# Four-layer hybrid network on one core: layer 1's input sent into the residual stream, the order at the begin of its MLP, and Fourier's row and last unit

## The chip, the cores and the metric

The kernel runs on one core of one Trainium2 chip. The metric is the time of one execution on the device, in microseconds; the time before is the median of three runs. The profile is that of one execution, and times inside it count from its first instruction.

## The reference

The input x is (4, 96, 64, 64) float32: batch, channels, image. As the kernel keeps it, it is 96 channels by 4 x 4096 tokens. Four layers follow each other. Layers 2 and 3 add their two parts to the stream of tokens.

```python
x = L0(x)   # two Mamba blocks, a 1x1 fusion with pooled channels, batch norm over (0, 2, 3), + input
x = L1(x)   # depthwise 7x7 conv, layer norm over channels, Linear(96, 384), GELU, Linear(384, 96), scale, + input
t = tokens(x)
t = t + linear_attention(ln(t))
t = t + qffn(ln(t))          # fp8 (e5m2) operands, f16 sums
t = t + fourier(ln(t))       # Linear(96, 192) + BN + ReLU, FFT over 4096 tokens, a complex gate with
                             # ReLU on both parts, inverse FFT, real part, Linear(192, 96), BN
t = t + qffn(ln(t))
```

## The kernel before

The program is one sequence of stages, each with pools of SBUF and PSUM buffers of its own. A pool that is closed gives its memory to the pools opened later; what is written there first waits for the last users of what lay there. Inside a stage the order of PE, DVE, ACT and POOL is the order of the program text (`manual_schedule(engines=...)`). SP, which issues all DMAs, isn't among those engines: a planner puts its instructions in an order of its own, and at run time its queue is strictly in that order, so a DMA that waits holds up all behind it.

**Layer 0** (0 to 2604 us) leaves its result, before the batch norm's scale, in a DRAM tensor `scratch` [96, 16384]. At its end it works out the batch norm's scale and shift, `osc` and `osh` (L614 to L622), in tiles of its pool.

**The turn of layer 1** (L727 to L757). The residual stream `t` [96, 16384] is a tile that lives from here to the end of the kernel; its memory was layer 0's. For each of 16 chunks of 1024 tokens, `tokens` loads a chunk of `scratch` into `o` (three buffers) and a chunk of x into `xr` (three buffers), ACT does o * osc + osh (L736), DVE adds xr and writes t (L737). `turn` then transposes the chunk, 128 tokens at a time, by a matmul with t as the stationary operand (96 rows by 128 columns) and the identity, 96 by 96, as the moving one (L744): eight matmuls a chunk, each of two records in the profile, since they are fp32. Four of them share a PSUM tile, which ACT (L750) or DVE (L748) copies into `xt`, the image with tokens in the partitions. `tokens` runs one chunk ahead of `turn`.

**The convolution** (L760 to L797, 2670 to 2790 us) takes 24 groups of four channels with weights `band` of 1 MB a group. In its ninth group `consts2` loads and prepares the constants of the later stages.

**Layer 1's MLP** (L805 to L870). `stats(k, d)` takes mean and variance of four rows of 128 tokens on DVE (bn_stats, bn_aggr; L810, L811), four such calls make a group k of 16 rows; `roots(k)` makes 1/sqrt on ACT with Ln and Exp; `back(i)` normalizes four rows (L824) and turns them back to channels on PE (L829), into `xc`; `hidden(i)` is the first linear with GELU (L838, L839), `out(i)` the second with the addition to t (L844, L847). There are 32 units i, in eight groups k. Before the first `hidden`, the kernel does the statistics and roots of groups 0 and 1 and `back` of units 0 to 3.

**Fourier** (`fourier`). A unit u is one image and one half of the 192 hidden channels: eight units. An iteration j takes a sixth part of a quarter of them, 6 groups of 4 channels, so that each unit has four iterations (`PER`), and the steps of several parts are staggered: `over_n1(j)` (first DFT, L1139), `over_n2(j-1)` (second DFT and gate, L1160 to L1179), `fold(j-2)`, `over_k2(j-3)` (first inverse DFT, L1208 to L1210, which fills the tile `bt[u]`). Frequency 64 is kept apart: `row64(u)` (L1216 to L1223) computes its 24 by 128 values, ACT copies them to `r`, a DMA writes them to DRAM (`d<-r`), and a second DMA loads them as row 64 of `bt[u]` (`bt<-d`). It is called in iteration 4u + 7. From iteration 4u + 8 on, the eight blocks of unit u are done, two an iteration: `over_k1` (second inverse DFT, L1230, with a table `gt` of 256 KB loaded for each block into one of two buffers, and ACT's copy to `ys`, L1232), then `w2` (the last linear, L1238, and the addition to t, L1242 or L1244). In the remaining places of an iteration stand the layer norm of the next image (`norm1`, `norm2`) and its first linear (`w1`, L1125), which are there only for the first three images. Most of the small matmuls share the two PSUM buffers of `misc`.

```python
                    if (j - 7) % PER == 0 and 0 <= (j - 7) // PER < len(units):
                        row64((j - 7) // PER)
```

The last FFN (`qffn`, 3838 us to the end) follows.

Of the kernel before, what the change touches and what calls it, by code (L numbers as in the profile page):

```python
# [9 lines left out]
F32 = mybir.dt.float32  # L10
# [8 lines left out]
B, C, HW, L = 4, 96, 64, 4096  # L19
# [31 lines left out]
class Net:  # L51
# [661 lines left out]
    def layer1(self, scratch, t):  # L713
# [4 lines left out]
        with ExitStack() as ctx:  # L718
            xpool = ctx.enter_context(tc.tile_pool(name="l1x", bufs=1))
            xt = xpool.tile([128, C, B, NR + 4], F32, name="xt")  # L720
            cb = xpool.tile([128, C], F32, name="cb")
            nc.sync.dma_start(cb, ins["c_b_row"].partition_broadcast(128))
            with (
                tc.manual_schedule(engines=engines),
                tc.tile_pool(name="l1a", bufs=1) as wk,
                tc.tile_pool(name="l1ap", bufs=1, space=PSUM) as psum,
            ):  # L727
                for at in (slice(0, 2), slice(NR + 2, NR + 4)):
                    nc.gpsimd.memset(xt[:, :, :, at], 0.0)
                def tokens(b, s):  # L730
                    at = slice(b * L + s * T, b * L + (s + 1) * T)
                    o = wk.tile([C, T], F32, name="o", tag="o", bufs=3)
                    nc.sync.dma_start(o, scratch[:, at])
                    xr = wk.tile([C, T], F32, name="xr", tag="xr", bufs=3)
                    nc.sync.dma_start(xr, ins["x"][b, :, s * T : (s + 1) * T])
                    nc.scalar.activation(o, o, AF.Identity, scale=self.osc, bias=self.osh)  # L736
                    nc.vector.tensor_add(t[:, at], o, xr)  # L737

                def turn(b, s):
                    for h in range(2):  # L740
                        ps = psum.tile([128, 4, C], F32, name="xt_ps", tag="xt", bufs=4)
                        for d in range(4):
                            a = b * L + s * T + (4 * h + d) * 128
                            nc.tensor.matmul(ps[:, d], t[:, a : a + 128], self.ident[:C, :C], start=True, stop=True)  # L744
                        r = 2 + s * (T // 128) + 4 * h
                        dst = xt[:, :, b, r : r + 4].rearrange("p c r -> p r c")
                        if h:
                            nc.vector.tensor_copy(dst, ps)  # L748
                        else:
                            nc.scalar.copy(dst, ps)  # L750

                chunks = [(b, s) for b in range(B) for s in range(NSC)]
                tokens(*chunks[0])
                for k, chunk in enumerate(chunks):
                    if k + 1 < len(chunks):
                        tokens(*chunks[k + 1])
                    turn(*chunk)  # L757

                def load(g):
                    w = wk.tile([128, GC, 4, 128], F32, name="band", tag="band", bufs=3)  # L760
                    nc.sync.dma_start(w, ins["band"][g])
                    return w

                def outer(g):

                    x2 = wk.tile([128, 2 * GC, B, NR], F32, name="x2", tag="x2", bufs=3)
                    at = slice(g * 2 * GC, (g + 1) * 2 * GC)
                    nc.gpsimd.tensor_copy(x2[:64], xt[:64, at, :, 4:])
                    nc.gpsimd.tensor_copy(x2[64:], xt[64:, at, :, :NR])
                    return x2  # L770

                def small(rows, cols):
                    ps = psum.tile([128, 4, C], F32, name="w_ps", tag="xt", bufs=4)
                    return ps.rearrange("p a c -> p (a c)")[:rows, :cols]

                x2 = [outer(0)]
                for g in range(C // GC):
                    if g == 8:
                        self.consts2(wk, small)
                    if g % 2 == 0 and g + 2 < C // GC:  # L780
                        x2.append(outer(g // 2 + 1))
                    w = load(g)
                    ps = psum.tile([128, GC, B, NR], F32, name="cv_ps", tag="cv", bufs=4)
                    for d in range(GC):
                        c = g * GC + d
                        for k, j in enumerate((1, 0, 2)):
                            nc.tensor.matmul(
                                ps[:, d], w[:, d, j], xt[:, c, :, 1 + j : 1 + j + NR], start=k == 0, stop=False
                            )
                        nc.tensor.matmul(ps[:, d], w[:, d, 3], x2[g // 2][:, g % 2 * GC + d], start=False, stop=True)  # L790
                    for d in range(GC):
                        c = g * GC + d
                        dst = xt[:, c, :, 2 : 2 + NR]
                        if g % 2:
                            nc.vector.tensor_scalar_add(dst, ps[:, d], cb[:, c : c + 1])
                        else:
                            nc.scalar.activation(dst, ps[:, d], AF.Identity, bias=cb[:, c : c + 1])  # L797
# [52 lines left out]
            n = NT // MB // 4  # L850
            with tc.manual_schedule(engines=engines):
                nc.scalar.preload_act_table_set(ACT_EXP_LN)
                for k in range(2):
                    for d in range(4):
                        stats(k, d)
                    roots(k)
                for d in range(4):
                    back(d)
                for k in range(n):
                    for d in range(4):  # L860
                        hidden(4 * k + d)
                        if k + 1 < n:
                            back(4 * k + 4 + d)
                        if k + 2 < n:
                            stats(k + 2, d)
                        if d:
                            out(4 * k + d - 1)
                    if k + 2 < n:
                        nc.scalar.preload_act_table_set(ACT_EXP_LN)
                        roots(k + 2)  # L870
                    out(4 * k + 3)
# [212 lines left out]
    def fourier(self, dram, t, h):  # L1084
# [5 lines left out]
        with ExitStack() as ctx:  # L1090
# [107 lines left out]
            def over_k2(i):  # L1198

                u, g = its[i]  # L1200
                z = zz.pop(i)
                if g == 0:
                    bt[u] = wk.tile([N1, N2, C], F32, name="bt", tag="bt", bufs=2)
                for e in range(0, G, 3):
                    ps = pln.tile([N1, 3, 128], F32, name="i1_ps", tag="i1", bufs=2)
                    for d in range(3):
                        zd = z[:, e + d].rearrange("p k m -> p (k m)")
                        nc.tensor.matmul(ps[:, d], zd[:, 64:], bc, start=True, stop=False)  # L1208
                        nc.tensor.matmul(ps[:, d], zd[:, :128], bs, start=False, stop=True)  # L1209
                    nc.scalar.copy(  # L1210
                        bt[u].rearrange("p n (g c) -> p g n c", c=4)[:, g + e : g + e + 3],
                        ps.rearrange("p g (n c) -> p g n c", c=4),
                    )

            def row64(u):
# [6 lines left out]
                nc.sync.dma_start(d.rearrange("o (n g c) -> g (o n) c", n=N2, c=4), r)  # L1222
                nc.sync.dma_start(bt[u][64:65].rearrange("p n c -> p (n c)"), d)  # L1223

            def over_k1(u, n, kept):
                gt = wk.tile([N1, 4, N1], F32, name="gt", tag="gt", bufs=2)
                nc.sync.dma_start(gt, ins["idft"][:, n : n + 4])
                ps = misc(C).rearrange("p (n a) -> p n a", n=4)
                for d in range(4):
                    nc.tensor.matmul(ps[:, d], bt[u][:, n + d], gt[:, d], start=True, stop=True)  # L1230
                kept[u, n] = wk.tile([C, MB], F32, name="ys", tag="ys", bufs=2)
                nc.scalar.copy(kept[u, n], ps.rearrange("p n a -> p (n a)"))  # L1232

            def w2(u, n, kept):

                b, half = units[u]
                ps = misc(C)
                nc.tensor.matmul(ps, self.a_w2[:, half, :], kept.pop((u, n)), start=True, stop=True)  # L1238
                ps = ps.rearrange("p (n a) -> p n a", n=4)
                td = ft[b][:, n : n + 4]  # L1240
# [6 lines left out]
            with tc.manual_schedule(engines=engines):  # L1247
                for n in range(0, N2, 2):
                    w1(0, n)
                kept, sq = {}, {}  # L1250
                for j in range(len(its) + 12):
                    ub, k = divmod(j - 2 * PER, PER)
                    blocks = [(ub, n) for n in (8 * k, 8 * k + 4)] if 0 <= ub < len(units) else []

# [9 lines left out]

                    if j < len(its):
                        over_n1(j)

                    if normed:
                        norm1(b, a, sq)
# [18 lines left out]
                        over_k2(j - 3)  # L1288
                    if normed:
                        norm2(a, sq)  # L1290
                    if (j - 7) % PER == 0 and 0 <= (j - 7) // PER < len(units):
                        row64((j - 7) // PER)
                    turn(len(tokens))
                    if blocks:
                        w2(*blocks[1], kept)
                    if normed and k == PER - 1:
                        norm2(a + MB, sq)


def build(tc, ins, out):  # L1300
# [155 lines left out]
```

## Time and profile before

| | |
|---|---|
| median of three runs | 3974.91 us (3973.95 to 3976.82) |
| the profiled execution | 3972.29 us, span 3970.5 us |
| granted TensorE clock, mean | 0.858 |
| layer 1: turn | 2614.6 to 2669.3 us |
| layer 1: convolution | 2670.4 to 2790.6 us |
| layer 1: MLP | 2790.7 to 3011.2 us |
| layer 3: Fourier, first L1139 to the last addition to t | 3318.1 to 3838.1 us |
| last FFN | 3838.1 us to the end |

The stages from the turn on follow each other on PE, which has work in nearly all of them; the table's times are those at which its first matmul begins or its last result is written. A row of the timeline gives start, duration, engine, line, operation, output and inputs, shapes, the count of instructions merged into it, and in brackets how long the engine was idle before it and what released it.

### The profile page before, as it was taken

To read this page: it belongs to the slowest core of one execution; us is meant where nothing else is said; L and a number is where in the kernel's file an instruction comes from. 1 tells how busy PE (TensorE), PEld (TensorE's weight loads), DVE (VectorE), ACT (ScalarE), POOL (GpSimd) and SP (SyncE) were. 2 spreads that over 40 slices of the span, in tenths; PEclk is the share of its full clock that TensorE was granted. 3 is DMA by queue.
4 is the path that set the end of the run, shared out by engine and by line. 5 is a ranking of instruction groups with operands and counts; after the bars stand their busy time and mean duration, and the time that the engine had idled before them with its cause. 6 is when DMAs were issued, how large, how long until landed. Compare 5 with 4: busy or idle time off the path is not lost. (4 is left out here: it accounts for less than half of the span.)

```text
span 3970.5 us, 45322 instructions
## 1 busy us (share of the span) xinstructions
PE 3291.6 (83%) x14174; PEld 1420.1 (36%) x14174; DVE 3155.9 (79%) x2772; ACT 2419.9 (61%) x4644; POOL 2912.9 (73%) x1443
## 2 busy tenths in 40 slices
PE   7888788888888778888878888677899998999878
PEld 3222222222222222222222222167445535666643
DVE  5999999999999999999999999941662384444539
ACT  4676667666666766677666666431345586655548
POOL 2999999999999999999999999911001064534417
PEclk8888888888887888788888888658899999999989
DMA  7567656756675667566666766566000000011111
GB/s 185 135 161 174 144 148 159 175 142 159 160 173 132 164 166 170 132 167 166 159 147 158 170 148 154 120 170 227 11 0 1 1 1 6 22 33 33 43 44 58
DMA packets 183291, 468.12 MB, mean 118 GB/s; under 512 B 53237, under 2 KB 55167, under 8 KB 179969
## 3 DMA queue, kind: packets, MB, share of 16 engines
q1 hardware_dynamic: 183048, 465.21, 47.1%
q8 instruction: 113, 1.85, 0.2%
q14 instruction: 130, 1.06, 0.1%
HBM read 391.53 MB, written 73.50 MB: 117 GB/s over the span
## 5 line engine op out<-in xcount | busy, mean ns | idle before, releaser
L496 POOL TENSOR_TENSOR hs<-hs,crep 128x1024 f32<-128x1024 f32 x768 | 1796.6, 2364 | 27.3 <-DVE hs L490 23.7
L454 PE MATMUL rep<-dbl,sel_b 32*128 32x512 f32 x1152 | 406.1, 781 | 464.1 <-DVE hs L490 433.4
L474 POOL TENSOR_TENSOR up<-udb,brep 128x1024 f32<-128x1024 f32 x256 | 605.1, 2364 | 8.5 <-DMA brep<-cd 8.5
L468 ACT ACTIVATE da<-ddb,nega 128x1024 f32<-128x1024 f32 x512 | 585.0, 1150 | 16.2 <-DVE hs L490 8.2
L468 ACT ACTIVATE dap<-ddb,nega 128x1024 f32<-128x1024 f32 x256 | 286.2, 1118 | 423.7 <-DVE hs L490 421.9
L515 PE MATMUL y<-hs,sel_r 128*32 128x512 f32 x3072 | 483.3, 689 | 6.5 <-POOL hs L496 6.4
L490 DVE TENSOR_TENSOR_SCAN hs<-da,state,rep 128x1024 f32<-128x1024 f32 x192 | 450.8, 2348 | 16.7
L490 DVE TENSOR_TENSOR_SCAN hs<-da,state,u 128x1024 f32<-128x1024 f32 x192 | 450.9, 2348 | 11.2 <-DVE u L486 1.4
L490 DVE TENSOR_TENSOR_SCAN hs<-dap,state,up 128x1024 f32<-128x1024 f32 x192 | 447.0, 2328 | 6.8 <-ACT dap L468 6.8
L454 PEld LDWEIGHTS rep<-dbl,sel_b 32*128 32x128 f32 x1152 | 109.0, 218 | 760.9 <-issue 512.8
L210 PE MATMUL ps<-n,w_x 97*64 97x512 f32 x1536 | 364.8, 617 | 9.4 <-ACT n L323 5.3
L486 DVE TENSOR_TENSOR u<-udb,rep 128x1024 f32<-128x1024 f32 x256 | 314.6, 1229 | 42.5 <-PE rep L454 11.3
L486 DVE TENSOR_TENSOR rep<-udb,rep 128x1024 f32<-128x1024 f32 x256 | 310.6, 1213 | 0.4
L1039 POOL CAST hq<-y 128x1536 fp8e5<-128x1536 f16 x64 | 93.9, 1467 | 253.7 <-issue 144.0
L210 PEld LDWEIGHTS ps<-n,w_x 97*64 97x64 f32 x1536 | 108.9, 140 | 257.5 <-issue 210.9
L515 PEld LDWEIGHTS y<-hs,sel_r 128*32 128x32 f32 x3072 | 66.9, 116 | 363.5 <-issue 195.8
L382 POOL TENSOR_TENSOR du<-delta,xc 128x512 f32<-128x512 f32 x96 | 122.6, 1277 | 67.4 <-ACT delta L366 52.2
L1178 POOL TENSOR_TENSOR av<-av,ec 128x780 f32<-128x780 f32 x32 | 58.8, 1837 | 150.1 <-ACT av L1175 150.1
L224 PE MATMUL ps<-xc,xproj 64*102 64x512 f32 x384 | 160.3, 998 | 3.5 <-ACT xc L344 3.5
L358 ACT COPY dbl<-ps 102x512 f32<-102x512 f32 x64 | 34.4, 589 | 207.1 <-PE ps L224 207.1
L911 POOL MEMSET h<- 1x4096 f32 x1 | 3.5, 3506 | 213.1 <-DVE n L824 213.1
L490 DVE TENSOR_TENSOR_SCAN hs<-da,rep 128x1024 f32<-128x1024 f32 x64 | 146.5, 2289 | 5.4
(256 smaller groups left out, 6492.9 us busy)
## 6 DMA issues: line engine op xcount, KB each, us to landing
ddb<-dd SPq DMA_DIRECT2D x768, 128.0 KB
udb<-ud SPq DMA_DIRECT2D x768, 128.0 KB
crep<-cd SPq DMA_DIRECT2D x512, 128.0 KB
brep<-cd SPq DMA_DIRECT2D x256, 128.0 KB
dd<-delta SPq DMA_DIRECT2D x64, 384.0 KB
ud<-du SPq DMA_DIRECT2D x192, 128.0 KB
band<-in_band SPq DMA_DIRECT2D x24, 1024.0 KB
gt<-in_idft SPq DMA_DIRECT2D x64, 256.0 KB
```

Source lines behind the costliest of these rows:

```text
L210: nc.tensor.matmul(ps[rows], w[:, 64 * p : 64 * p + 64], rhs[:, at.start + shift : at.stop + shift], start=k == 0, stop=k == len(ws) - 1, ...
L224: nc.tensor.matmul(ps, w[rows, p], x[rows, p], start=start and p == 0, stop=p == 2)
L382: nc.gpsimd.tensor_mul(u, m["delta"][:, of], m["xc"][:, of])
L454: nc.tensor.matmul(x[:, at], sel_b[rows, order[t][1]], made[k]["dbl"][rows, at], start=True, stop=True)
L468: nc.scalar.activation(da, made[k]["dd", h, j], AF.Exp, scale=nega[:, col : col + 1])
L474: nc.gpsimd.tensor_mul(u, made[k]["ud", h, j], made[k]["brep", g])
L486: nc.vector.tensor_mul(u, made[k]["ud", h, j], x)
L490: nc.vector.tensor_tensor_scan(hs[:, 1:], made[k].pop(("da", t)), u, 0.0 if s == 0 else st, ALU.mult, ALU.add)
L496: nc.gpsimd.tensor_mul(hs[:, :T], hs[:, 1:], made[k]["crep", order[t][1]])
L515: nc.tensor.matmul(made[k]["y", p][row : row + 32], sel_r, made[k]["hs", t][:, at], start=False, stop=True, skip_group_check=True,)
L1039: nc.gpsimd.tensor_copy(q, y2, saturate=False)
L1178: nc.gpsimd.tensor_add(v[:, 2:4], v[:, 0:2], ec)
```

## The change

In the turn, x is loaded into t itself, one image (1536 KB) a DMA: images 0 to 2 ahead of all chunks in the program text, image 3 in the fourth chunk's `tokens`. `xr` is gone, DVE adds o to t in place, and o has six buffers. The transposing matmul takes all 128 columns of the identity's first 96 rows; the PSUM tile is one of 4 x 128 columns, and the copies read 96 of each 128.

In the MLP, only the statistics and roots of group 0 and `back(0)` stand before the first `hidden`. `back` runs two units ahead, and in group 0 the statistics of groups 1 and 2 are done at two calls a unit; the roots of group 1 come behind the third `hidden`.

In Fourier, `row64(u)` is called in iteration 4u + 6. The last unit's blocks stand in a loop of their own at the end, with `over_k1` of a block ahead of `w2` of the one before it; the tables are loaded in two DMAs of 1 MB into buffers of `hh`, called in iterations 25 and 29, and from then on each block whose table is there reads it (two blocks of unit 4, all of units 5, 6 and 7) in place of loading `gt`; the last unit's `w2` uses the PSUM buffers of `over_k2` in place of `misc`.

```diff
+            def input_of(b):
+                nc.sync.dma_start(t[:, b * L : (b + 1) * L], ins["x"][b])
+
+            for b in range(B - 1):
+                input_of(b)
...
-                    o = wk.tile([C, T], F32, name="o", tag="o", bufs=3)
+                    o = wk.tile([C, T], F32, name="o", tag="o", bufs=6)
                     nc.sync.dma_start(o, scratch[:, at])
-                    xr = wk.tile([C, T], F32, name="xr", tag="xr", bufs=3)
-                    nc.sync.dma_start(xr, ins["x"][b, :, s * T : (s + 1) * T])
+                    if (b, s) == (0, NSC - 1):
+                        input_of(B - 1)
                     nc.scalar.activation(o, o, AF.Identity, scale=self.osc, bias=self.osh)
-                    nc.vector.tensor_add(t[:, at], o, xr)
+                    nc.vector.tensor_add(t[:, at], o, t[:, at])
...
-                        ps = psum.tile([128, 4, C], F32, name="xt_ps", tag="xt", bufs=4)
+                        ps = psum.tile([128, 4, 128], F32, name="xt_ps", tag="xt", bufs=4)
...
-                            nc.tensor.matmul(ps[:, d], t[:, a : a + 128], self.ident[:C, :C], start=True, stop=True)
+                            nc.tensor.matmul(ps[:, d], t[:, a : a + 128], self.ident[:C], start=True, stop=True)
...
-                            nc.vector.tensor_copy(dst, ps)
+                            nc.vector.tensor_copy(dst, ps[:, :, :C])
                         else:
-                            nc.scalar.copy(dst, ps)
+                            nc.scalar.copy(dst, ps[:, :, :C])
...
-                for k in range(2):
-                    for d in range(4):
-                        stats(k, d)
-                    roots(k)
                 for d in range(4):
-                    back(d)
+                    stats(0, d)
+                roots(0)
+                back(0)
                 for k in range(n):
                     for d in range(4):
-                        hidden(4 * k + d)
-                        if k + 1 < n:
-                            back(4 * k + 4 + d)
-                        if k + 2 < n:
+                        i = 4 * k + d
+                        hidden(i)
+                        if k == 0 and d == 2:
+                            nc.scalar.preload_act_table_set(ACT_EXP_LN)
+                            roots(1)
+                        for i2 in (1, 2) if i == 0 else (i + 2,):
+                            if i2 < 4 * n:
+                                back(i2)
+
+                        if k == 0:
+                            for d2 in (2 * (d % 2), 2 * (d % 2) + 1):
+                                stats(1 + d // 2, d2)
+                        elif k + 2 < n:
                             stats(k + 2, d)
                         if d:
-                            out(4 * k + d - 1)
+                            out(i - 1)
...
+            late = {}
+
+            def fetch(k):
+
+                g = wk.tile([N1, CG, N2, 4], F32, name="hh", tag="hh", bufs=3)
+                g = g.rearrange("p g n c -> p (g n c)")[:, : N2 // 2 * N1].rearrange("p (n a) -> p n a", n=N2 // 2)
+                nc.sync.dma_start(g, ins["idft"][:, k * N2 // 2 : (k + 1) * N2 // 2])
+                for n in range(0, N2 // 2, 4):
+                    late[k * N2 // 2 + n] = g[:, n : n + 4]
+
             def over_k1(u, n, kept):
-                gt = wk.tile([N1, 4, N1], F32, name="gt", tag="gt", bufs=2)
-                nc.sync.dma_start(gt, ins["idft"][:, n : n + 4])
+                if n in late:
+                    gt = late[n]
+                else:
+                    gt = wk.tile([N1, 4, N1], F32, name="gt", tag="gt", bufs=2)
+                    nc.sync.dma_start(gt, ins["idft"][:, n : n + 4])
...
-                ps = misc(C)
+                if u < len(units) - 1:
+                    ps = misc(C)
+                else:
+                    ps = pln.tile([N1, 4, 128], F32, name="i1_ps", tag="i1", bufs=2)[:C].rearrange("p n a -> p (n a)")
...
-                for j in range(len(its) + 12):
+                for j in range(len(its) + 4):
...
                     if j < len(its):
                         over_n1(j)
+                    if j in (len(its) - 7, len(its) - 3):
+                        fetch((j - len(its) + 7) // 4)
...
-                    if (j - 7) % PER == 0 and 0 <= (j - 7) // PER < len(units):
-                        row64((j - 7) // PER)
+                    if (j - 6) % PER == 0 and 0 <= (j - 6) // PER < len(units):
+                        row64((j - 6) // PER)
...
+                last = [(len(units) - 1, n) for n in range(0, N2, 4)]
+                for k, block in enumerate(last):
+                    over_k1(*block, kept)
+                    if k:
+                        w2(*last[k - 1], kept)
+                w2(*last[-1], kept)
```

More of the change, by code (lines that the diff above doesn't have):

```diff
@@ L772, in small @@
                 def small(rows, cols):
-                    ps = psum.tile([128, 4, C], F32, name="w_ps", tag="xt", bufs=4)
+                    ps = psum.tile([128, 4, 128], F32, name="w_ps", tag="xt", bufs=4)
                     return ps.rearrange("p a c -> p (a c)")[:rows, :cols]
@@ L1204, in over_k2 @@
                 for e in range(0, G, 3):
-                    ps = pln.tile([N1, 3, 128], F32, name="i1_ps", tag="i1", bufs=2)
+                    ps = pln.tile([N1, 4, 128], F32, name="i1_ps", tag="i1", bufs=2)[:, :3]
                     for d in range(3):
```

## The prediction

> **What bounds the kernel now.** I read the page first (busy shares, the 40 slices), then the busy time by stage, then the timeline around each edit, engine by engine.
>
> ```profile
> PE 3291.6 (83%) x14174; PEld 1420.1 (36%) x14174; DVE 3155.9 (79%) x2772; ACT 2419.9 (61%) x4644; POOL 2912.9 (73%) x1443
> PEclk8888888888887888788888888658899999999989
> ```
>
> The shares say little: layer 0, 0 to 2604 us, is bound by DVE and POOL and is not edited. What the change touches lies behind 2604, where PE leads; slices 27 and 28 have a granted clock of 0.6 and 0.5. By stage:
>
> ```profile
> 2614.50:2640.00 25.50, 25.42 (x119) 25.42 (x120) 13.74 (x16) 14.52 (x15) 0.00 (x0) 0.50 1.02 262
> 2740.00:2780.00 40.00, 40.00 (x360) 40.00 (x360) 6.19 (x23) 6.87 (x24) 9.81 (x10) 1.00 0.87 293
> ```
>
> Columns after the length: busy PE, PEld, DVE, ACT, POOL, then clock, DMA share, GB/s. The first row is layer 1's turn (L744): PE is full, but at half clock, and the DMA engines are full too, at 262 GB/s. The second is the convolution: PE full at full clock. The turn runs from 2614.58 to 2669.3, 256 matmul records in 54.7 us, 213 ns each.
>
> In Fourier, the waits of PE at the first block of a unit:
>
> ```profile
> 3477.94 1.94 PE L1230 MATMUL m_ps<-gt,bt 128*96 128x128 f32 x8 [2.95 <-DMA bt<-d]
> ...
> 3605.41 1.99 PE L1230 MATMUL m_ps<-gt,bt 128*96 128x128 f32 x8 [3.20 <-issue]
> ...
> 3719.93 1.60 PE L1230 MATMUL m_ps<-gt,bt 128*96 128x128 f32 x8 [3.55 <-DMA bt<-d]
> ...
> 3770.96 1.99 PE L1230 MATMUL m_ps<-gt,bt 128*96 128x128 f32 x8 [4.89 <-DMA bt<-d]
> ...
> 3812.57 1.99 PE L1230 MATMUL m_ps<-gt,bt 128*96 128x128 f32 x8 [4.73 <-issue]
> ```
>
> Brackets: idle before, and who ended it. With 0.83 (3543.39) and 1.66 (3670.59) these are seven waits, 21.8 us, for the row of frequency 64, which goes through DRAM (d<-r, then bt<-d). And the eight matmuls take 1.94 to 1.99 us there, 1.04 elsewhere: the clock has fallen. The last unit, in PE's timeline:
>
> ```profile
> 3822.44 1.10 PE L1238 MATMUL m_ps<-ys,a_w2s 96*96 96x512 f32 x2 [0.72 <-ACT ys L1232]
> 3823.38 1.04 PE L1230 MATMUL m_ps<-gt,bt 128*96 128x128 f32 x8
> 3825.14 1.10 PE L1238 MATMUL m_ps<-ys,a_w2s 96*96 96x512 f32 x2 [0.73 <-ACT ys L1232]
> ```
>
> A block is 2.70 us: PE, ACT's copy, PE, with nothing between. And the begin of the MLP:
>
> ```profile
> 2804.67 1.99 PE L829 MATMUL tp_ps<-ident,n 128*96 128x128 f32 x8 [15.28 <-DVE n L824]
> ```
>
> PE waits for 32 rows of statistics.
>
> **What the Trainium skill says.** "TensorE: Matmul & The Clock Gate", section "What's actually happening": the array's clock is half until it has been busy for a window of about 3.4 us, and falls back after an idle one. The trace agrees: the convolution goes from 0.51 (2670 to 2676) to 1.00, and waits of 2.95 us and more are followed by half speed; also waits of under 1 us at 3485, so the rule is not the whole of it. The same page, "LDWEIGHTS (loading the stationary operand)": the load's time goes by the columns of the stationary tile. Here that is 128, and L744's 213 ns (96 moving columns) is the pace of L829 at half clock with 128 moving columns (8 in 1.99 us): 128 columns should cost L744 nothing. "DMA: Bandwidth & Descriptors", section "Why a DMA increments its semaphore by 16 and not by 1": 96 rows go over all 16 engines, 97 over one. Trace: o and xr (96 rows) reach 262 GB/s, bn1_rows (97 rows, 291 KB, issued at 2695.72, used at 2717.29) takes 21.6 us.
>
> **Part A, input and turn.** Gone: 16 transfers xr of 384 KB. New: four of 1536 KB into t, by the same queue, SP's. Same bytes: 12.6 MB in all. SP is not ordered by hand; t stands where layer 0's pool stood, which is read until L622 (2609.4). So I take SP's order as: six o (six buffers now), then x0 to x3, then o6. In front of x0 are cb, the last store and six o, 2.8 MB; from 2605.5 at 260 GB/s to 2616.3; x0 6 us, to 2622.3; landing takes 1 to 2 more (xr0 was seen to land only at 2613.2, behind 1.2 MB). First add and matmul at about 2625, 10 us later than now. x1 to x3 come at 2630, 2636, 2642, o6, stuck behind them, at 2643.5. Chunks 0 to 5 are through by then (at full clock 1.8 us each); chunk 6 waits. From there a chunk costs ACT 1.23 + 0.80 = 2.03 us, DVE 1.20 + 0.80 = 2.00, PE 16 x 0.111 = 1.78 (the convolution's pitch): nine more to 2662, the last matmul at about 2665, against 2669.3: **-4**. The convolution begins at a warmer clock: its first group took 5.8 us, of which 2.2 wait for POOL, 3.58 is the later pace: **-1**. Bounds: at 310 GB/s, seen from 2607 to 2608.5, x0 lands 4 us sooner and o6 7 sooner: -12. At half clock: 2625 + 54.7 = 2679.7: +10. That the clock rises isn't shown for this shape; I take it, since 128 moving columns leave no hole in the array's stream where 96 leave a quarter. Queued behind: the bands, issued after the last o; 3.1 MB at 416 GB/s (2660 to 2664) is 7.6 us, hidden by the rest of the turn.
>
> **Part B, begin of the MLP.** DVE ends the convolution at 2790.6; 16 statistics x 0.42 = 6.7, roots with two table loads 3.15: first matmul at 2801.3, 3.4 sooner. Then PE waits more: 0.9 for the first xc, 1.2 before the third turn, 2.0 before the fourth (eight statistics, 3.4 us, lie in front on DVE), 3.3 before the fifth (table load 1.28, roots 0.53, behind the third unit's Gelu): 7.4, against 3.6 now. Three turns get full clock, 1.1 each, but 3.3 us of idleness may take the clock away again, 2 to 3 us. PE's work, 32 x (0.87 + 6 x 0.86) = 193 us, is the same. Sum: -3.4 + 3.8 - 3.3 + 2.5: **0**, bounds -4 and +3.
>
> **Part C, the row.** row64 moves from iteration 4u+7 to 4u+6, behind the unit's last over_k2; with it PE's four matmuls, ACT's copy and both DMAs. Their chain, 5.6 us (d<-r 3.0, bt<-d 2.4), then has an iteration of 11.6 to 14.7 us as cover, in the last unit two w2 and two blocks, 6 us. SP: both stand between gt transfers whose blocks are one iteration off. What a wait costs shows in the iterations, from L1139 to L1139:
>
> ```profile
> 3473.48 1.50 PE L1139 MATMUL s_ps<-dft,hh 128*128 128x130 f32 x12
> ...
> 3495.48 1.50 PE L1139 MATMUL s_ps<-dft,hh 128*128 128x130 f32 x12
> ...
> 3510.14 1.50 PE L1139 MATMUL s_ps<-dft,hh 128*128 128x130 f32 x12
> ```
>
> 22.0 us with the wait, 14.66 without. I leave 0.65 for small waits: 6.7 for unit 1, 6.5 for unit 3 (21.82). Unit 5: 15.58 against 11.58, 4.0. Units 2 and 4: 0.8 each. Unit 6: 4.89 and 2.1 of half clock, less 0.6 since ACT's fold then comes in front: 6.4. Unit 7: 4.6 and 2.7 of half clock (0.95, 0.92, 0.87): 7.3. Sum 32.5, less 1.5 for what comes next (ACT's ys): **-31**. Bounds: the bare waits, -20, and -34.
>
> **Part D, last unit.** over_k1 of a block now runs ahead of w2 of the one before: 0.87 + 0.86 = 1.73 us a block on PE, over ACT's 0.58 + 0.15 and DVE's 1.15. 8 x (2.70 - 1.73) = 7.8, less 0.3 at the ends: **-7.5**. It needs gt early: two loads of 1 MB (2.6 us each at 416 GB/s), called in iterations 25 and 29, in hh buffers last read in 23 and 27. Every block from then on whose part is there uses it: two of unit 4, all of units 5 to 7, so 26 loads of 256 KB go, 6.8 MB for 2. On SP the two hold up a row or gt for 2.6 us at most, inside the slack. The first readers stand in iterations 25 and 30; if SP puts a load late, PE waits up to 4 us there (2.6 and a landing); SP may put it as early as the buffer is free, so 0. The last FFN then begins at a warmer clock: its first iterations take 4.4 us with 2.02 for L887, 1.10 later: 0 to -4, I take **-1**.
>
> Other edits (PSUM shapes of 128 columns, one bank as before): nothing.
>
> **Sum.** -5 + 0 - 31 - 7.5 - 1 = -44.5. From the profiled execution's 3972.3 (span 3970.5) 3927.8; the median, 3974.9, lies 2.6 higher: **3930**.
>
> **Rivals.**
> 1. The turn stays at half clock: part A +10 in place of -5: 3945. For it: 54 us at 0.50 with PE full; against: the convolution, of 128 columns, goes to 1.00.
> 2. Only the waits go, the half clock stays (as at 3485, without a long wait): part C -20: 3941. Against: the iterations without a row wait have 1.00.
> 3. Long rows are quick, 310 GB/s, and the clock rises: part A -12: 3923.
> 4. Slower: t's rows are 16 KB, a length that no load around here has. bn1_rows shows what few engines mean: 291 KB in 21.6 us, 13.5 GB/s on one. If x fell to few engines, its 6.3 MB would hold all o behind it: on one engine 466 us, some 4370 in all. It decides from the point where the 6.3 MB take the 24 us planned here and the 40 us gained elsewhere: 98 GB/s, seven such engines. Against it: xr, also 96 rows, runs at 262 GB/s.
>
> **Numbers.** Likeliest 0.62; rival 1 0.13; 2 0.12; 3 0.09; 4 0.04. A measurement here can tell some 0.2%, 8 us. All but rival 4 are faster by more; I leave 0.03 for no change. The range 3912 to 3949 holds the first, rivals 1 to 3, and their bounds in part.
>
> **What would show it.** Right: L744 at 111 ns a record and a clock near 1.00 in the turn, its first matmul near 2625 and a wait of a few us at the seventh chunk; L1230 with no wait for bt<-d; iterations 12 and 20 under 16 us; blocks of the last unit of 1.75 us. Wrong: L744 at 213 ns; PE waiting over 3 us at L1230 for gt or bt; the first matmul of the turn after 2635; an MLP that ends over 3 us sooner or later against its begin.

## The result, and the profile after

The changed kernel takes 3938.60 us (median of four runs, 3937.12 to 3940.83), beside 3974.43 us of the kernel before: ratio 0.9916, interval 0.9896 to 0.9935. That is 33 us less by the ratio (26 to 41 by its interval) and 36 by the two medians; the forecast was 45, with 26 to 63 as its range. The profiled execution takes 3937.12 us (span 3935.4), 35.2 less than that of before. The total lies in the range; several of its parts don't lie where they were put, and one gain was not in the sum at all.

The page of the kernel after, its busy times and clock slices:

```profile
PE 3262.6 (83%) x14174; PEld 1392.3 (35%) x14174; DVE 3156.6 (80%) x2772; ACT 2418.7 (61%) x4644; POOL 2912.1 (74%) x1443
PEclk8788878888888888888898888768899999999999
```

PE has the same 14174 matmuls in 29 us less busy time, 17.7 us of it in the turn, where they had run at half clock. The slices around the turn stand at 7 and 6 where 6 and 5 stood.

By stages, from the two traces (the end of each is where the next one's first matmul starts, for the convolution the start of its last matmul, for Fourier the end of the last addition to t):

| stage | before, us | after, us | difference |
|---|---|---|---|
| to the end of the turn (of it, layer 0 is 1.5 shorter) | 2670.4 | 2674.6 | +4.2 |
| convolution | 118.7 | 114.0 | -4.7 |
| layer 1's MLP | 222.1 | 222.8 | +0.7 |
| attention, first FFN | 306.8 | 299.8 | -7.0 |
| Fourier | 520.0 | 491.3 | -28.7 |
| last FFN | 132.4 | 132.8 | +0.4 |

**The turn.** PE's timeline of the kernel after (start, duration, line, in brackets the wait and its releaser):

```profile
2621.19 8.20 PE L750 MATMUL xt_ps<-ident,t 96*128 96x128 f32 x48 [18.40 <-DVE t L743]
2637.58 3.79 PE L750 MATMUL xt_ps<-ident,t 96*128 96x128 f32 x16 [8.19 <-DVE t L743]
2645.91 7.81 PE L750 MATMUL xt_ps<-ident,t 96*128 96x128 f32 x48 [4.54 <-DVE t L743]
2654.23 3.84 PE L750 MATMUL xt_ps<-ident,t 96*128 96x128 f32 x32 [0.52 <-DVE t L743]
```

And SP's queue, where a row's duration reaches over all issues merged into it:

```profile
2605.31 0.94 SPq L739 DMA_DIRECT2D o<-scratch  x2
2609.87 1.26 SPq L725 DMA_DIRECT2D t<-in_x  x3
2611.17 0.42 SPq L739 DMA_DIRECT2D o<-scratch  x1
2611.64 0.69 SPq L725 DMA_DIRECT2D t<-in_x  x1
2612.36 46.49 SPq L739 DMA_DIRECT2D o<-scratch  x12
```

Three chunks of o (the first was issued at 2603.38) are ahead of x; then three images, 4.7 MB, then the fourth o, then the last image, and then the other twelve o. The fourth chunk (16 records) waits until 2637.58, the fifth until 2645.91. Behind that, the last two rows are quick: 32 records in 3.84 us and a wait of half a microsecond. In the table of windows the clock is back:

```profile
2655.00:2673.00 18.00, 15.97 (x136) 15.21 (x135) 15.25 (x16) 13.72 (x16) 0.00 (x0) 1.00 0.85 282
```

**The convolution.** Its waits, as total, times and longest, in the kernel after:

```profile
PE w_ps L703 <- DVE bn_d L699: 10.0, 1, 10.0
PE cv_ps L793 <- DMA band<-in_band: 9.6, 3, 8.7
```

Before, the first of these is 25.7 us. bn_rows is issued at 2672.21 now, at 2695.72 before, because SP's order puts the constants right behind the first bands; in return one band comes 8.7 us late.

**The attention,** which no edit touches, begins at full clock in the kernel after, and did not before. First the timeline after, then before, some 1.8 us after the first matmul of the stage in both:

```profile
3013.21 1.10 PE L900 MATMUL v_ps<-sq,ones 96*96 96x512 f32 x2 [0.74 <-ACT sq L896]
3016.23 1.10 PE L900 MATMUL v_ps<-sq,ones 96*96 96x512 f32 x2 [1.06 <-ACT sq L896]
```

```profile
3013.06 1.35 PE L887 MATMUL v_ps<-sq,ones 96*96 96x512 f32 x2 [0.74 <-ACT sq L883]
3016.80 2.02 PE L887 MATMUL v_ps<-sq,ones 96*96 96x512 f32 x2 [0.68 <-ACT sq L883]
```

**Fourier.** No wait for bt<-d is left in the trace. But iterations 12 and 20, from L1152 to L1152, take 18.52 and 19.54 us; an iteration without a wait takes 14.66. All engines of iteration 12 in the timeline after:

```profile
3469.44 1.04 PE L1256 MATMUL m_ps<-gt,bt 128*96 128x128 f32 x8
...
3471.03 1.27 POOL L1129 TENSOR_TENSOR h<-h,ln_rs 96x512 f32<-96x512 f32 x1 [1.46 <-ACT ln_rs L1128]
...
3471.81 2.72 DVE L1203 SCALAR_TENSOR_TENSOR zz<-av 128x384 f32<-128x384 f32 x1 [0.27 <-ACT av L1198]
3472.26 1.86 POOL L1164 TENSOR_TENSOR f<-p,p 128x390 f32<-128x390 f32 x2
...
3474.54 0.55 DVE L1203 SCALAR_TENSOR_TENSOR zz<-av 128x384 f32<-128x384 f32 x1
...
3475.12 0.52 ACT L1209 ACTIVATE zz<-zz 128x384 f32<-128x384 f32 x1 [3.41 <-DVE zz L1203]
3475.55 0.56 ACT L1258 COPY ys<-m_ps 96x512 f32<-96x512 f32 x1
...
3476.16 1.68 PE L1267 MATMUL m_ps<-ys,a_w2s 96*96 96x512 f32 x2 [3.06 <-ACT ys L1258]
3477.64 1.91 PE L1256 MATMUL m_ps<-gt,bt 128*96 128x128 f32 x8
```

To be read from below: w2 waits 3.06 us for ys; the matmul that ys copies ended at 3470.48, but ACT stood in front of it at the fold's last step, 3.41 us, for DVE's zz; of two equal zz, the first took 2.72 us and the second 0.55; and while the first ran, POOL ran too, until 3474.12. The first zz had started 0.45 us before POOL's two f, and still ended only after them. The last row shows what follows a wait of 3 us: eight matmuls at 1.91 us in place of 1.04.

These are figures of one execution. Two other profiles below hold the same Fourier program: there iterations 12 and 20 take 20.10 and 19.50 us, and 20.29 and 18.45, and Fourier takes 492.7 and 494.4 us. Three profiles with the Fourier program of before have 520.1, 516.5 and 517.1. A difference of 2 us in one of these iterations, or of 3 us in the stage, can therefore not be put down to an edit.

**The last unit** runs as forecast, a block every 1.73 us:

```profile
3789.68 1.04 PE L1256 MATMUL m_ps<-hh,bt 128*96 128x128 f32 x8
3790.55 1.02 PE L1267 MATMUL i_ps<-ys,a_w2s 96*96 96x512 f32 x2
3791.41 1.04 PE L1256 MATMUL m_ps<-hh,bt 128*96 128x128 f32 x8
```

### The profile page after: what moved, and what is told of

Its sections match the earlier page's. It is cut to its first block, busy times and chain, and to the rows that moved or that the text cites. A ratio compares the mean times of both kernels' runs of the same rounds, so it can differ in the third digit from the quotient of the medians.

```text
span 3935.4 us, 45230 instructions
## 1 busy us (share of the span) xinstructions
PE 3262.6 (83%) x14174; PEld 1392.3 (35%) x14174; DVE 3156.6 (80%) x2772; ACT 2418.7 (61%) x4644; POOL 2912.1 (74%) x1443
```

## The experiments

Twelve further kernels ran in three rounds, each with the kernel before beside it (its medians 3972.30, 3971.97, 3972.89).

| kernel | median, us | ratio to before, interval |
|---|---|---|
| 128 columns alone | 3964.35 | 0.9981 (0.9974 to 0.9987) |
| input part alone | 3977.43 | 1.0013 (1.0006 to 1.0019) |
| MLP's begin alone | 3965.53 | 0.9985 (0.9979 to 0.9992) |
| row64 alone | 3956.60 | 0.9959 (0.9947 to 0.9970) |
| last unit alone | 3957.73 | 0.9965 (0.9953 to 0.9978) |
| after, without the input part | 3928.73 | 0.9897 (0.9882 to 0.9913) |
| after, old begin of the MLP | 3946.58 | 0.9931 (0.9918 to 0.9944) |
| after, POOL's sums moved | 3935.60 | 0.9908 (0.9894 to 0.9922) |
| after, over_k1 ahead of fold | 3928.88 | 0.9895 (0.9880 to 0.9911) |
| after, fold ahead of over_n1 | 3929.36 | 0.9896 (0.9878 to 0.9914) |
| no input part, over_k1 ahead of fold | 3915.37 | 0.9860 (0.9846 to 0.9875) |
| no input part, order over_k1, fold, over_n1 | 3895.21 | 0.9809 (0.9791 to 0.9826) |

The five parts alone sum to -40 us by their medians, which the interval of the whole change, 26 to 41 us, holds. A kernel that differs from the changed one by 10 us or less has an interval that overlaps with the changed one's; there the reading rests on the stages of the profiles.

### Which half of part A costs, which gains?

The kernel before with 128 columns only:

```diff
-ps = psum.tile([128, 4, C], F32, name="xt_ps", tag="xt", bufs=4)
+ps = psum.tile([128, 4, 128], F32, name="xt_ps", tag="xt", bufs=4)
-nc.tensor.matmul(ps[:, d], t[:, a : a + 128], self.ident[:C, :C], start=True, stop=True)
+nc.tensor.matmul(ps[:, d], t[:, a : a + 128], self.ident[:C], start=True, stop=True)
-nc.vector.tensor_copy(dst, ps)
+nc.vector.tensor_copy(dst, ps[:, :, :C])
...
```

> The kernel before with only the 128 columns in the turn (xr and o by chunks, three buffers each, as before). Theory (the clock rises with the filled array): L744 falls from 213 ns to some 111 ns a record, PE needs 1.8 us a chunk and waits for each pair of loads, 768 KB at 262 GB/s, 3.0 us; the last matmul of the turn moves from 2669 to about 2662, the total by -7 us (-4 to -12). Rival (the waits of 1 us a chunk keep the clock at half): 213 ns a record and no change, 0.

Measured: 8 us less. Its timeline shows chunks of 2.05 us with waits of 0.2 to 1.0 between them, and one wait of 2.08:

```profile
2624.76 2.05 PE L744 MATMUL xt_ps<-ident,t 96*128 96x128 f32 x16 [0.82 <-DVE t L737]
...
2634.68 8.62 PE L744 MATMUL xt_ps<-ident,t 96*128 96x128 f32 x48 [2.08 <-DVE t L737]
```

The turn takes 46.3 us to the start of its last matmul (54.5 before). The clock rises and stays up through the waits of up to 1 us (0.94 granted from 2615 to 2634.6); after the one of 2.08 us the next three chunks took 8.62 us at 0.64. The rival with half clock is out. The width of the PSUM tile went with the 128 columns, and no run parts the two.

The kernel before with the input part only (x into t, six o, DVE in place), 96 columns:

```diff
...
-xr = wk.tile([C, T], F32, name="xr", tag="xr", bufs=3)
-nc.sync.dma_start(xr, ins["x"][b, :, s * T : (s + 1) * T])
+if (b, s) == (0, NSC - 1):
+    input_of(B - 1)
-nc.vector.tensor_add(t[:, at], o, xr)
+nc.vector.tensor_add(t[:, at], o, t[:, at])
```

> The kernel before with only the input part: x straight into t in four loads, six buffers for o, 96 columns in the turn. Theory (x held in front of the fifth o is what starves the turn, and the early loads of the constants shorten the stall in the convolution): the fifth chunk starts near 2637, the sixth near 2646, then 11 chunks at half clock, 3.4 us each, to about 2683, +14 us at the turn's end; the convolution 6 us shorter; total +8 us (+3 to +12). Rival (the shorter convolution belongs to the warm clock of the 128 columns): +14.

Measured: 5 us more (interval 2 to 8). Fourth chunk at 2636.17, fifth at 2644.41, and from there half clock to the end:

```profile
2636.17 3.73 PE L749 MATMUL xt_ps<-ident,t 96*128 96x96 f32 x16 [5.36 <-DVE t L742]
2644.41 41.27 PE L749 MATMUL xt_ps<-ident,t 96*128 96x96 f32 x192 [4.50 <-DVE t L742]
```

The turn ends 16 us later than before, and the convolution is 14.5 us shorter (104.2 us): its wait at w_ps is 10.4 us here too, and at least 24.9 us in every kernel without the input part. So the early constants belong to the input part. What the large loads cost the turn, the early constants nearly pay back.

The changed kernel with the loads of before (x by chunks into xr, three buffers of each):

> The changed kernel without its input part: x by chunks into xr as before, three buffers, but 128 columns. Theory (the loads of x held in front of o cost what the faster matmul wins, less what the early constants give back): turn as in the run of the 128 columns alone, 46 us, its end some 14 us sooner than in the changed kernel, the convolution 6 us longer; total -8 us against the changed kernel (-5 to -11), near 3930. If the clock at the begin of the attention follows from the new begin of the MLP, L900's first matmuls take 1.10 us here, not 1.4 to 2.0; if it is chance, either may come. Rival (parts don't add): within 3 us of the changed kernel.

Measured: 3928.73, ten less than the changed kernel; the intervals of the two ratios overlap. The run of the input part alone is slower than before by more than its interval, and a pair further down (over_k1 ahead of fold, with and without the input part, 3928.88 and 3915.37) has intervals that don't overlap: the sign is safe, the size, 5 to 14 us, is not. The profiled execution of this kernel was its longest, 3939.1: its attention fell back to half clock and took 307.0 us, its loads ran at 237 GB/s, and its turn took 52.2 us, against 270 to 284 GB/s and 46.3 in the run of the 128 columns, with the same program there. The other two profiles with that program have 52.6 and 50.9 us, so 46.3 is the short one of four. Nothing in these traces says why; the run of the 128 columns was on another chip than the other three.

### Does the begin of the MLP do anything?

The kernel before with the new begin of the MLP alone:

> The kernel before with only the new begin of layer 1's MLP. Theory (the first product comes 11 us sooner, but PE waits for the statistics and the roots between the next ones and falls to half clock): the time from the last product of the convolution to the last one of the MLP changes by +2 us (0 to +3), total 0 to +3. Rival (the prediction's value, a gain that pays for its waits): 0, down to -4.

Measured: 7 us less (interval 3 to 8), which neither expected. The MLP itself is as the theory has it, 222.4 us against 222.1. The gain lies in the attention: 300.5 us to the first L1146 of Fourier, where the kernel before has 306.8, since its first matmuls run at full clock. (In this profile the last FFN is 4 us shorter too; see the last unit below.)

The changed kernel with the old begin of the MLP, that is, this part undone:

> The changed kernel with the old begin of layer 1's MLP. Theory (the new begin brings the clock at the begin of the attention, not the MLP itself): the time from the last product of the convolution to the first of the attention within 1 us of the changed kernel's, L900's first matmuls at 1.4 to 2.0 us in place of 1.10, the first L1152 6.5 us later after the MLP's end; +6 us in the median (+4 to +8). Rival (that clock is chance): +-2 in the median, and L900 at 1.10 about as often as not.

Measured: 8 us more by the medians, 6 by the ratios. Its attention takes 307.7 us, where the changed kernel has 299.8. Its timeline:

```profile
3011.48 2.00 PE L893 MATMUL v_ps<-sq,ones 96*96 96x512 f32 x2 [0.74 <-ACT sq L889]
```

Of fourteen profiles, all six with the old begin have half clock there, and seven of eight with the new one have full clock in the first matmuls (the exception is the kernel without the input part, where it falls one matmul later). So the new begin does bring it, 200 us ahead of the place where it shows. How it does so is argued here and not shown: the Trainium skill, "TensorE: Matmul & The Clock Gate", section "What's actually happening", says that the monitor's windows run freely, some 3.4 us each. While the clock is half, PE's progress hangs on where a window ends; the waits of the begin, 0.8, 1.1, 1.9 and 3.1 us, set how PE stands to the windows, and from the MLP's middle on it has no wait over 0.3 us that could shift this. The waits at the begin of the attention, 0.84 and 0.74 us, then fall in one window or in two. No run here shows the windows themselves, so this stays open.

### Where did part C's gain go?

The kernel before with row64 an iteration earlier, alone:

> The kernel before with only row64 an iteration earlier. Theory (the wait for the row is gone, but ACT's copy of ys, which stands behind the fold of two iterations before, comes out as the next wait of 3 us in iterations 12 and 20, with half clock behind it): units 1 and 3 gain 2 to 3 us each, not 6.7 and 6.5; in all -20 us (-15 to -24). Rival (that wait comes from the other edits): iterations 12 and 20 fall under 16 us, in all -29 to -32.

Measured: 16 us less. Iterations 12 and 20 take 20.16 and 20.09 us (22.00 and 21.82 before), and PE's waits name ys, 3.1 us in each, with no other edit in place. The rival is out: the wait comes with the moved row.

Is it DVE's zz beside POOL? The Trainium skill, "SBUF — State Buffer", section "Who interferes with whom", says that a DVE operation with two operands in SBUF and a POOL operation that reads SBUF can't run together, the second one waits until the first is done. zz has two such operands. (The trace above differs in one point: POOL's f began after zz, and zz waited for them as well.) The changed kernel with one thing moved, where `sums` issues the two sums f that over_n1 issued itself:

```diff
 if j < len(its):
-    over_n1(j)
+    sums = over_n1(j)
+    if j not in (12, 20):
+        sums()
...
 if 1 <= j < len(its) + 1:
     over_n2(j - 1)
+if j in (12, 20):
+    sums()
```

> The changed kernel with one thing moved: in iterations 12 and 20 POOL's sums f stand behind its sums av. Theory (DVE's zz, which reads two operands from SBUF, stands still while POOL works on SBUF): the first zz falls from 2.72 us to 0.6 to 1.6 (only POOL's last product h still runs at its start), PE's wait of 3.06 us for ys to about 1.5, iterations 12 and 20 by 1.5 to 4 us each; total -3 to -7 us against the changed kernel. Rival (zz is slow there for another reason): 2.7 us as before, iterations 12 and 20 at 18.5 and 19.5 us.

Measured, in iteration 12:

```profile
3472.11 1.27 POOL L1129 TENSOR_TENSOR h<-h,ln_rs 96x512 f32<-96x512 f32 x1 [1.46 <-ACT ln_rs L1128]
3472.89 0.91 DVE L1207 SCALAR_TENSOR_TENSOR zz<-av 128x384 f32<-128x384 f32 x1 [0.26 <-ACT av L1202]
...
3475.43 1.10 PE L1271 MATMUL m_ps<-ys,a_w2s 96*96 96x512 f32 x2 [1.24 <-ACT ys L1262]
```

zz ends 0.42 us after POOL's h, as it ended 0.41 us after POOL's f in the changed kernel; the wait is 1.24 in place of 3.06, and the clock stays (1.10 in place of 1.68). Iterations 12 and 20 take 16.64 and 16.63 us, below the 18.45 to 20.29 of the three profiles with POOL's old order. Fourier is 3.4 us shorter (487.9), the median 3 us lower, which alone would show nothing; the durations of the rows carry the verdict, and they agree with what the skill's page says.

Is ACT's order enough? The changed kernel with two calls exchanged:

```diff
+if blocks:
+    over_k1(*blocks[0], kept)
 if 2 <= j < len(its) + 2:
     fold(j - 2)
-if blocks:
-    over_k1(*blocks[0], kept)
```

> The changed kernel with one pair of calls exchanged: the first over_k1 of an iteration stands ahead of fold, so that ACT copies ys before it waits for DVE's zz. Theory (the waits that took the place of the row waits are ACT's order): iterations 12 and 20 fall from 18.5 and 19.5 us to under 15.5, the wait of 4.03 us in iteration 33 goes, the waits of 1.22 us an iteration from 25 on go; -18 us against the changed kernel (-12 to -23), total near 3919. Rival (DVE's zz, stretched to 2.7 us beside POOL, is the limit, and the wait comes back at over_k2 or the next product): -5 or less.

Measured: 10 us less, not 18, and iterations 12 and 20 are no better, 20.08 and 20.06. ys is on time, but the wait stands one step on:

```profile
3471.12 2.25 DVE L1203 SCALAR_TENSOR_TENSOR zz<-av 128x384 f32<-128x384 f32 x1 [0.84 <-ACT av L1198]
...
3474.80 1.12 DVE L1273 TENSOR_TENSOR t<-t,m_ps 96x512 f32<-96x512 f32 x1
3476.07 1.52 PE L1138 MATMUL m_ps<-a_w,h 97*128 97x192 f32 x4 [2.50 <-DVE t L1273]
```

The next matmul needs the PSUM buffer of w2, which DVE's addition to t empties, behind the delayed zz. Here the rival of this run was right. The gain came from elsewhere: iterations 13 to 15 and 21 to 23, 0.9 us each, and the wait of 4.03 us for ys that the changed kernel has in iteration 33 (the kernel before has one of 4.46 there).

And DVE's order? The changed kernel with fold ahead of over_n1, so that zz stands before the products p:

> The changed kernel with fold ahead of over_n1, at the start of an iteration. Theory (the waits that took the place of the row waits come from where DVE's zz stands, behind the products p and beside POOL's sums f): zz takes 0.55 to 1 us in iterations 12 and 20, ys is no longer late, both fall under 16.5 us from 18.5 and 19.5; in iterations from 24 on p waits for zz instead, within its slack; -6 us against the changed kernel (-3 to -12). Rival (the wait moves to p and from there to the next second DFT): iterations 13 and on grow, 0 or worse.

Measured: 9 us less; iterations 12 and 20 take 16.17 and 16.18 us, and no zz of the whole stage takes more than 0.99 us. The late iterations, 24 to 30, take 10.1 to 11.3 us in place of 11.6 to 12.3. Part of the gain is lost in iterations 9, 10, 17 and 18, which take 1.3 to 4.6 us longer, since the layer norm's h is late on DVE; in iteration 9:

```profile
3424.89 1.83 PE L1125 MATMUL m_ps<-ln_sq,ones 96*96 96x512 f32 x2 [2.54 <-DVE h L1119]
```

The changed kernel waits 0.85 us there.

Both, without the input part. First over_k1 ahead of fold only:

> Both: the changed kernel without its input part and with over_k1 ahead of fold. Theory: the gains add, -26 us against the changed kernel, near 3911 (3905 to 3920), with full clock at the begin of the attention as in the two runs with the new begin of the MLP. Rival: no better than the better one of the two by more than 3 us.

Measured: 3915.37; the gains of the two edits add within what can be told. Then the order over_k1, fold, over_n1:

```diff
+if blocks:
+    over_k1(*blocks[0], kept)
+if 2 <= j < len(its) + 2:
+    fold(j - 2)
 if j < len(its):
     over_n1(j)
...
-if 2 <= j < len(its) + 2:
-    fold(j - 2)
-if blocks:
-    over_k1(*blocks[0], kept)
```

> The changed kernel without its input part, and with the order over_k1, fold, over_n1 in an iteration. Theory: ys is first on ACT and zz first on DVE, so both waits go: -8 us for the turn, -6 to -12 more for Fourier, near 3912, at or below the 3915 of the run with over_k1 ahead of fold alone. Rival: DVE's p is late now and the second DFT waits, above 3920.

Measured: 3895.21, 17 us below what was expected, 43 below the changed kernel, 78 below the kernel before. Fourier takes 455.0 us (491.3 in the changed kernel). The two orders are worth more together than alone (-9.4 and -9.7 us of Fourier each, -36.3 both). The surplus lies in iterations 9 to 12 and 16 to 20: there over_k1 first alone takes 1.3 and 0.7 us longer, which is within the spread, fold first alone 3.1 and 2.2 longer, and both together 3.7 and 5.7 less. Each alone still has PE waiting for DVE there, for t in the one and for h in the other; with both, iterations 9 to 11, 17 and 18 have no wait over 0.3 us. Why the new place of over_k1 ends the wait for h stays open. In a late iteration PE doesn't wait for ys, and it takes 10.13 us in place of 11.58, a gain that fold first brings for the most part alone:

```profile
3669.37 1.02 PE L1261 MATMUL m_ps<-ys,a_w2s 96*96 96x512 f32 x2
3670.23 1.04 PE L1250 MATMUL m_ps<-gt,bt 128*96 128x128 f32 x8
```

### The last unit alone

> The kernel before with only the last unit's loop and the two loads of 1 MB. Theory: its blocks come at 1.73 us in place of 2.70, seven of them, and the wait of 4.7 us for the row of unit 7 stays in front of the first: -7 us (-5 to -9). Rival (the loads of gt that are gone also free the waits for the rows of units 4 to 6): those waits, 1.66, 3.55 and 4.89 us, shrink by over 1 us each, -10 or better.

Measured: 14 us less, twice the expectation, but Fourier itself is 8 us shorter, as the theory has it, and the waits for the rows of units 4 to 6 are as before (1.9, 3.6 and 4.8 us): the rival is out. Another 4 us of the profiled execution are the last FFN's: its first matmuls run at full clock there (L887 at 1.07 and 1.10 us). They do so in four of the fourteen profiles of this case, two of them of kernels with the last unit's loop and the moved row, one with neither; that looks like chance, and the runs don't settle it.

## Why the prediction was right in the sum, by its own steps

**Part A (-5 forecast).** Measured -0.5 for turn and convolution together, from +4.2 and -4.7; +1 without the 1.5 us by which layer 0, which nobody edited, was shorter. The clock rose as taken (32 records in 3.84 us, some 120 ns each, against 213), and the run of the 128 columns alone shows -8 us. The first matmul came at 2621.2, sooner than the 2625 forecast. The step that failed is SP's order: "six o, then x0 to x3, then o6". SP had three o, three images, one o, the last image. Thus the waits, 8.2 and 4.5 us, hit the fourth and fifth chunk, and twelve chunks were left at 2645.9, not ten at 2643.5; at 2.3 us each, not 2.03, they ended at 2673.7, not 2665. The second term that was missing is what else SP's new order moved: bn_rows 23 us sooner, 7 us less waiting in the convolution, of which the prediction had nothing. Its -1 for a warmer clock came true: the first group takes 5.24 us in place of 6.74, where the prediction had read 5.8.

**Part B (0).** Right in its place: +0.7 us. The first matmul came 3.3 us sooner against the convolution's end (forecast 3.4), the waits were 0.8, 1.1, 1.9 and 3.1 us (forecast 0.9, 1.2, 2.0 and 3.3), and half clock came after the last one. What failed is the border drawn around it: the same edit was worth 7 us at the begin of the attention, for which the prediction has no term.

**Part C (-31).** The mechanism was right; every row wait went. But the row alone took 16 us off, where 31 were forecast. The term mis-sized is "less 1.5 for what comes next (ACT's ys)". Against before, iterations 10 to 12 gain 3.3 us for 6.7 forecast, 18 to 20 gain 2.1 for 6.5; 14 to 16 and 22 to 24 gain 0 and 0.6 for 0.8 each; 26 to 28 gain 4.0, as forecast; iterations 0 to 9, which have no row wait, took 1.2 longer, and 1.7 and 1.3 in the runs of the row alone and without the input part. In the two large ones ys came out 3 us late, and with it the half clock that had been booked as saved. The cover of a wait was read from PE's side only. Before, ACT's zz had also waited 2.44 us in iteration 12, below PE's wait for the row; when PE came sooner, so did the collision of DVE and POOL.

**Part D (-7.5, next FFN -1).** A block takes 1.73 us as worked out; from iteration 30 to the end of Fourier 20.0 us went, where units 6 and 7 of part C and this part make 21.2. The loads of 1 MB delayed nothing. The next FFN began at half clock as before: 0.4 longer in place of 1 shorter.

**The sum.** -44.5 forecast, -35.2 measured on the profiled execution. Part A lacks 4.5 us, part B 0.7, Fourier 9.8 and the FFN 1.4; the attention gives 7.0. The central value was off by 9 us, and the range held it because it reached to rival 2, "only the waits go", at 3941. That rival came nearest in its number: units 1 and 3 kept their half clock, but behind a new wait rather than without one. Rivals 1, 3 and 4 are out: the clock rose, and the loads moved at 228 GB/s in the window of the turn's begin (2614.5 to 2640), where 310 and under 98 were asked for. There was luck in the total: without the 7 us of the attention, which no step forecast, the median would have been near 3946, and the miss 16 us instead of 9. (The prediction's chances add up to 1.00 before the 0.03 that it leaves for no change.)

## What to carry to other kernels

A wait that is removed is worth the distance to the next one that would have held the same engine: look, inside the old wait, at which other engines were also late there, in this case ACT behind DVE behind POOL. When loads are made larger or moved to a free buffer, work out the order of the queue that issues them, with all that stands behind, before pricing the bytes: here two images, 3.1 MB that nobody needed yet, stood in front of the fourth chunk's 0.4 MB, and PE waited 8.2 us; the last image in front of the fifth chunk's made it wait 4.5 more. When one exchange only shifts a wait to the next engine of a chain, try the exchange that moves both, since the gain comes with the second.

## What the runs showed of the hardware

- A DVE operation of two SBUF operands, 0.55 us alone, takes 2.72 us when it starts while POOL works, and ends some 0.4 us after POOL's last operation, though two of the POOL operations began after it; with POOL's sums moved it takes 0.91.
- A stream of nothing but matmuls with 96 moving columns stayed at half clock for 54 us without a gap; with 128 moving columns (and a wider PSUM tile) it went to full clock and kept it through waits of 0.8 us every 2.9 us, but not through one of 2.08 us. It is no rule for every place: in the attention of the kernel before, groups of eight matmuls with 97 moving columns, between wider ones, ran at full clock, 0.9 us a group (granted clock 1.00 from 3060 to 3130 us).
- The order at the begin of one stage went with the clock at the begin of the next stage, 200 us later, in 13 of 14 profiles; undone or done alone, it moved that stage by 6 to 8 us. How is not shown.
- The same loads, 384 KB each in the same program, ran at 237 GB/s in one execution and at 270 to 284 in another, on another chip, and the turn took 52.2 and 46.3 us.
